# A four-stage transformer block on one core: one pool of eight PSUM banks in place of pools of five and three, with new due times for the planner

## The chip, the core and the metric

The kernel runs on one core of one Trainium2 chip. A core has a matrix engine (TensorE, PE in the profile, its weight loads shown apart as PEld), a vector engine (VectorE, DVE), a scalar engine (ScalarE, ACT), a general engine (GpSimd, POOL) and SyncE (SP), which here only issues DMAs. Each engine works through its own queue in order and waits for others by semaphores. TensorE writes its results to PSUM, which here is used as eight banks of 128 partitions by 512 fp32 values; VectorE and ScalarE read them from there. The metric is the device time of one launch in microseconds (us), taken as the median of several runs.

## The reference

The input x is 8 batches of 512 tokens by 512 features, in fp32. Four stages follow, each with the sandwich `x = x + layernorm(stage(layernorm(x)))`:

```
a0: scores = einsum('bci,bcj->bij', x, x); softmax; context = einsum('bij,bcj->bci', w, x)
f0: einsum('btd,rde->bte', x, factors) / sqrt(8) + bias          # factors: 8 of 512x512
a1: h = norm_scale * x / (rms(x) + eps) * split_scale
    q, k, v = h @ Wq.T, h @ Wk.T, h @ Wv.T       # 8 heads of 64, k and v for 2 groups
    x + softmax(q k^T / 8) v @ Wo.T
f1: g = (x @ gate_w.T) * gate_s;  u = (x @ up_w.T) * up_s         # 1408 wide, ternary weights
    (silu(g) * u) @ down_w.T * down_s
```

In f0 the eight factors act on the same input, so their sum is one matrix of 512x512.

## The kernel before

**Work and tiling.** A batch is four tiles of 128 tokens by 512 features. `layers` builds, for each of the eight batches, the operations of `stage_attn0` (a0), `stage_ffn0` (f0), `stage_attn1` (a1) and `stage_ffn1` (f1). The fp32 stages use fp32 matmuls. In f1 the weights are ternary and exact in the fp32r format, so each activation is split into two fp32r parts (`hl`, made by ScalarE at L1101 and VectorE at L1110), and both parts are multiplied (L1167 for gate and up, L1235 for down). At the start of the program the weights' low bits are tested (`look_at_low_bits`); with the given data a second, plain copy of the layers is skipped.

**Shapes of the array.** Most matmuls use the whole 128x128 array. Transposes of pairs of tiles (L637), transposes of attention weights (L977) and attention scores (L946) use 64-row halves of it, two at a time, and write two banks; the product of attention weights with v (L1008) uses 64-column halves. The program's names for these are "128x128", "128x128r" (fp32r), "64x128" and "128x64".

**The order.** `Recorder.add` takes each operation down with its engine, an estimated duration, what it reads and writes, and a due time. `Recorder.issue` then plays the whole program through: it keeps a clock for each engine and takes operations one at a time, and the order in which it takes them is the order in which they stand in the engines' queues on the chip. For each engine it looks at the operations that could start within `SLACK` of the earliest one, and takes the one with the lowest due time:

```
                pick = min(
                    (p + stay * self.change(e, state.get(e), op.state), n, s, op)
                    for s, p, n, op in able
                    if s <= first + slack[e]
                )
```

Here `change` is the planner's price of another array shape (on PE 0.21 us from "64x128" or "128x64" into "128x128r", 0.09 into any other, nothing between "128x128" and "128x128r") or of another function table (1.3 us on ACT), and it is part of the planned start `s` as well. `stay` is `STAY` of the engine. Due times are in units of one batch: `due` adds the stage's entry in `DUE`, the number of the batch, a `SHIFT` for the first three and last two batches, and a slope for each step within the stage (`e1` and `h1` are the attention and FFN of the last batch, which work in halves). `SMALL` is taken off the due time of operations under 0.3 us.

**Buffers.** A `Buf` gets a place of its tag when its first operation is taken, and gives it back when the last one is. If no place is free the operation can't be taken yet. PSUM has two tags: `f` with five banks, for a0, f0, a1, all transposes and one product of the half steps, and `g` with three, for gate, up and down products. Gate and up weights come in slices of 256 KB into four places of tag `wgu`, issued from POOL's queue (L389); x, factors and attention weights are issued from SP (L368). The product pair of one slice ends in a sigmoid on ScalarE (L1187) and two operations on VectorE (L1197, L1206), the last of which releases the second bank.

**Softmax.** A row takes VectorE's maximum (L575), ScalarE's exponential (L582), VectorE's reciprocal (L592) and its scaling (L599). A layernorm takes two statistics operations on VectorE (L518, L523), two small ones on POOL (L527, L534) and the normalisation on VectorE (L542).

Of the kernel before, what the change touches and what calls it, by code (L numbers as in the profile page):

```python
# [10 lines left out]
F32 = mybir.dt.float32  # L11
# [6 lines left out]
P = 128  # L18
# [35 lines left out]
class Recorder:  # L54
# [20 lines left out]
    def add(self, eng, dur, fn, reads=(), writes=(), room=(), after=(), state=None, lat=None):  # L75
# [5 lines left out]
        op.lat = self.LAT[eng] if lat is None else lat  # L81
        op.prio = self.prio - (SMALL if dur < 0.3 else 0.0)
        op.succ, op.wait, op.ready = [], 0, 0.0
# [34 lines left out]
    def issue(self, places, slack):  # L118
# [24 lines left out]
        while left:  # L143
            best = None
            for e, ops in ready.items():
# [3 lines left out]
                first = min(able)[0]  # L149
                stay = STAY.get(e, 0.0)  # L150
                pick = min(
# [99 lines left out]
def layers(  # L251
# [24 lines left out]
    B, S, D = x_in.shape  # L276
# [4 lines left out]
    NT = S // P  # L281
# [8 lines left out]
    psum = ctx.enter_context(tc.tile_pool(name="ps", bufs=1, space=bass.MemoryType.PSUM))  # L290
# [7 lines left out]
    def columns(tag, n, width):  # L298

        t = one(tag, [P, n * width])  # L300
        return [t[:, ts(i, width)] for i in range(n)]
# [21 lines left out]
        "ve": columns("ve", 24, 1),  # L323
        "rstd": columns("rstd", 24, 1),
        "s1": columns("s1", 24, 1),
        "f": [psum.tile([P, D], F32, tag=f"f{i}", name=f"f{i}") for i in range(5)],
        "g": [psum.tile([P, D], F32, tag=f"g{i}", name=f"g{i}") for i in range(3)],
    }
    ident = one("ident", [P, P])
    make_identity(nc, ident)  # L330
# [21 lines left out]
    def when(kind, b, *steps):  # L352

        rec.prio = due(kind, b if b < B // 2 else b - B, B, *steps)
# [17 lines left out]
    fsum = Fixed("fsum", BIG)  # L372
# [7 lines left out]
    wd = Fixed("wd", [P, NI, D], FAST)  # L380
# [125 lines left out]
    def whole(b):  # L506
        return (b, lambda t: t[:, :])
# [32 lines left out]
    def normalize(dst, src, mv, rstd, us=0.55, room=(), after=()):  # L540
        def go():
            nc.vector.tensor_scalar(  # L542
                ap(dst), ap(src), mv.t[:, 0:1], rstd.t[:, :], ALU.subtract, ALU.mult
            )

        add("DVE", us, go, reads=[ref(src), mv, rstd], writes=[ref(dst)], room=room, after=after)
# [570 lines left out]
    def stage_ffn1(x, b, after):  # L1117
# [11 lines left out]
        for q, (toks, its) in enumerate(rounds):  # L1129
            cut = slice(toks[0] * P, (toks[-1] + 1) * P)  # L1130
            mine = [(x_, (t, hf)) for x_ in xs for t in toks for hf in range(2)]
            took = (0.69, 0.75) if len(toks) == NT else (0.4, 0.42)
            for t in toks:
                if t in known:
                    continue
                known.add(t)
                when(kind + "norm", b, t - toks[0], q)
                if t % 2 == 0:
                    pair = [Buf("row"), Buf("row")]
                xn = pair[t % 2]  # L1140
                mv, rstd = moments(whole(x[t]))
                normalize(whole(xn), whole(x[t]), mv, rstd, room=[*xs, *pair])
                rows.append(whole(xn))
                if t % 2 == 0:
                    continue
                pts, into, bank = transpose_two(xs[0], t - 1, rows[-2:], room=xs, copy=False)
                for hf in range(2):
                    dsts = [((x_, (t, hf)), into(hf)) for x_ in xs]
                    in_parts(dsts, lambda hf=hf, bank=bank: bank(hf), [pts[hf]], 0.6, also=(t - 1, hf))

            for c, (lo, hi) in enumerate(CUTS):
                for it in range(lo, hi):
                    if it not in its:
                        continue
                    when(kind + "gate", b, it, q)
                    sig = Buf("sig" if len(toks) == NT else "e")
                    hd = (hds[c], lambda tt, k=it - lo, cut=cut: tt[:, k, cut])
                    pg, pu = Buf("g"), Buf("g" if len(toks) == NT else "f")
                    wg = load_slice("wgu", gate_t, it, after=after)
                    wu = load_slice("wgu", up_t, it, after=after)  # L1160

                    def product(bank, w, cut=cut):
                        def go():
                            n = 0
                            for kt in range(KT):
                                for d in xs:
                                    nc.tensor.matmul(  # L1167
                                        bank.t[:, cut],
                                        w.t[:, kt, :],
                                        d.t[:, kt, cut],  # L1170
                                        start=(n == 0),
                                        stop=(n == KT * len(xs) - 1),
                                    )
                                    n += 1

                        return go


                    us = PASS * KT * len(xs) * len(toks) / NT
                    mm(pg, us, product(pg, wg), [wg, *mine], room=[hds[c]], state=array)  # L1180
                    products.append(mm(pu, us, product(pu, wu), [wu, *mine], state=array))
                    gsc = lambda it=it: gs.t[:, it : it + 1]
                    usc = lambda it=it: us_.t[:, it : it + 1]
                    add(
                        "ACT",
                        took[0],
                        lambda sig=sig, pg=pg, gsc=gsc, cut=cut: nc.scalar.activation(  # L1187
                            sig.t[:, cut], pg.t[:, cut], AF.Sigmoid, scale=gsc()
                        ),
                        reads=[pg, gs],  # L1190
                        writes=[sig],
                        state="sig",
                    )
                    add(
                        "DVE",
                        took[1],
                        lambda sig=sig, pg=pg, gsc=gsc, cut=cut: nc.vector.scalar_tensor_tensor(  # L1197
                            sig.t[:, cut], pg.t[:, cut], gsc(), sig.t[:, cut], ALU.mult, ALU.mult
                        ),
                        reads=[pg, gs],  # L1200
                        writes=[sig],
                    )
                    add(
                        "DVE",
                        took[1],
                        lambda sig=sig, pu=pu, usc=usc, hd=hd, cut=cut: nc.vector.scalar_tensor_tensor(  # L1206
                            ap(hd), pu.t[:, cut], usc(), sig.t[:, cut], ALU.mult, ALU.mult
                        ),
                        reads=[pu, us_, sig],
                        writes=[(hds[c], (it - lo, u)) for u in range(2) if 2 * u in toks],  # L1210
                    )
        for t in range(NT):
            po = Buf("g")
            for c, (lo, hi) in enumerate(CUTS):
                when(kind + "down", b, t, c)
                n = hi - lo
# [55 lines left out]
    for b in range(B):  # L1272
        x = [Buf("x") for _ in range(NT)]
# [12 lines left out]
    with tc.manual_schedule():  # L1286
        rec.issue(places, SLACK)

# [1 line left out]


DUE = {
    "x": (-2.3159,),
    "fsum": (0.3241, 0.0093),
    "scales": (-1.7199,),
    "wd": (0.1588,),
    "low": (0.6749, 1.0396),
    "a0.norm": (0.5999,),
    "a0.row": (-0.0925, 0.0032),
    "a0.out": (0.61, 0.0014),  # L1300
    "f0": (-0.1636, 0.1196),
    "a1.norm": (0.4967, -0.0502),
    "a1.kv": (-1.8548,),
    "a1.q": (0.5431, 0.0591),
    "a1.row": (0.5193, 0.0765, 0.0294, -0.0187),
    "a1.mix": (1.4217, -0.005, 0.0185),
    "a1.out": (1.6212, -0.0623),
    "e1.row": (0.2868, -0.0014, 0.037, -0.0171),
    "e1.mix": (-2.6369, 42.9472, 0.5484),
    "e1.out": (1.0638, 0.0783, 0.0342),  # L1310
    "f1.norm": (-0.7064, 0.0727),
    "f1.gate": (1.5542, 0.001),
    "f1.down": (1.7443, 0.1972, 0.0317),
    "h1.norm": (1.3712, -0.2677, 0.0575),
    "h1.gate": (2.6762, 0.5726, 5.4087),
    "h1.down": (1.5597, -2.5384, 1.2861),
}

SHIFT = {
    ("a0", 0): -0.0077,  # L1320
    ("f0", 0): 0.3239,
    ("f1", 0): -0.0869,
    ("a0", 1): -0.1846,
    ("a1", 1): -0.1496,
    ("f0", 1): -0.3089,
    ("x", 1): -0.0564,
    ("a0", 2): 0.3238,
    ("a1", 2): -0.0022,
    ("f0", 2): 0.0353,
    ("f1", 2): -0.0044,  # L1330
    ("x", 2): 0.0586,
    ("a1", -2): -0.0031,
    ("f0", -2): 0.1802,
    ("f1", -2): -0.0946,
    ("x", -2): -0.3405,
    ("a0", -1): -0.0302,
    ("a1", -1): -0.1096,
    ("f0", -1): -0.4004,
    ("f1", -1): -0.1873,
    ("x", -1): 0.1371,  # L1340
}

STAY = {"PE": 0.0901}

SLACK = {"PE": 0.123, "ACT": 0.0528, "DVE": 0.0772, "POOL": 1.2606, "SP": 0.1357}

SMALL = 0.8159
FSUM_POOL = (0, 3)
EARLY = (-1,)
FEW = 4  # L1350
# [54 lines left out]
```

## Time and profile before

| | |
|---|---|
| median of 3 runs | 1515.19 us (1515.05 to 1517.9) |
| the profiled execution: its own time | 1514.31 us |
| the profiled execution: its span, first to last instruction | 1512.4 us |
| mean granted TensorE clock | 0.998 |
| PE busy | 1468.9 us |
| DVE busy | 1050.5 us |
| ACT busy | 665.7 us |
| POOL busy | 586.2 us |
| chain that ended last: share of PE | 86% |
| DMA moved | 108.04 MB |

Busy time of PE is the time in which at least one matmul is under way. Matmuls overlap at their ends, so that in a timeline the time that a group takes is read from its start to the start of the next one, not from its own length, which includes an end that runs beside the next. The kernel before is one that keeps PE busy for almost the whole span; the other engines have gaps.

### The profile page before, as it was taken

The numbers are of one execution on the slowest core, as the hardware profiler recorded it, in microseconds if no ns is written. First come the engines' busy times: TensorE is split into PE (matmuls) and PEld (weight loads), VectorE is DVE, ScalarE is ACT, GpSimd is POOL, SyncE is SP. The second block draws the span as 40 slices with busy tenths as digits, with TensorE's granted clock in tenths as the row PEclk, the third lists the DMA queues.
The fourth block names the chain that finished last, engine by engine and source line by source line (L and its number), as shares of the span: only waits on it lengthen the run. The fifth ranks groups of instructions, "written<-read, shape, count | busy, mean of one in ns | idle before, by whom it ended". The sixth has DMA issues, their size and how long they took to land.

```text
span 1512.4 us, 23159 instructions
## 1 busy us (share of the span) xinstructions
PE 1468.9 (97%) x8562; PEld 907.7 (60%) x8562; DVE 1050.5 (69%) x2227; ACT 665.7 (44%) x1422; POOL 586.2 (39%) x884
## 2 busy tenths in 40 slices
PE   5899999999999999999999999999999999999997
PEld 3444547765666556665576656665566655666575
DVE  6999875678567685586846868467774757758745
ACT  2225746441266423763246622465225652266412
POOL 6662132137512374033730347213571116611451
PEclk9999999999999999999999999999999999999999
DMA  9523124212431224212151122411233102420291
GB/s 336 158 82 108 29 64 97 50 57 58 85 68 43 46 53 97 51 42 71 28 106 35 57 56 47 101 36 43 57 70 84 36 15 63 88 59 29 49 168 38
DMA packets 156698, 108.04 MB, mean 71 GB/s; under 512 B 7072, under 2 KB 137120, under 8 KB 156576
## 3 DMA queue, kind: packets, MB, share of 16 engines
q0 software_dynamic: 98736, 51.13, 17.8%
q1 hardware_dynamic: 57840, 55.34, 11.9%
q8 instruction: 70, 1.15, 0.3%
q14 instruction: 52, 0.43, 0.1%
HBM read 98.06 MB, written 8.39 MB: 70 GB/s over the span
## 4 chain that ended last, share of the span: by engine, by line
PE 86%; DVE 5%; POOL 4%; issue 2%; DMA 1%; ACT 1%; SPq 0%; POOLq 0%; DVEq 0%; ACTq 0%
PE g L1167 21%; PE g L1235 11%; PE f L1008 8%; PE f L946 8%; PE f L917 7%; PE f L1034 7%; PE f L977 5%; PE f L726 5%; PE f L748 5%; PE f L695 4%; PE f L637 2%; PE f L898 2%; PE f L887 2%; POOL rstd L534 1%; DVE row L542 1%
## 5 line engine op out<-in xcount | busy, mean ns | idle before, releaser
L1167 PE MATMUL g<-hl,wgu 128*128 128x512 f32 (+1 forms) x1408 | 338.6, 394 | 2.7 <-DMA wgu<-in_gate_t 1.6
L1167 PEld LDWEIGHTS g<-hl,wgu 128*128 128x128 f32 x1408 | 256.0, 188 | 70.9 <-DVE s L575 10.6
L527 POOL TENSOR_SCALAR ve<-mv 128x1 f32<-128x1 f32 x224 | 67.8, 304 | 593.1 <-DVE mv L523 587.0
L575 DVE TENSOR_REDUCE s<-f 128x1 f32<-128x512 f32 x288 | 184.8, 683 | 97.7 <-PE f L946 57.2
L582 ACT ACTIVATE e<-f,s 128x512 f32<-128x512 f32 x288 | 196.0, 688 | 79.3 <-DVE s L575 76.2
L561 POOL TENSOR_TENSOR x<-x,z 128x512 f32<-128x512 f32 x120 | 165.3, 1382 | 47.0 <-DVE z L542 40.0
L1235 PE MATMUL g<-wd,hl 128*128 128x512 f32 x704 | 175.3, 402 | 1.4 <-DVE hl L1110 1.4
L989 ACT COPY big<-f 128x512 f32<-128x512 f32 x256 | 135.9, 593 | 80.6 <-PE f L977 80.1
L1235 PEld LDWEIGHTS g<-wd,hl 128*128 128x128 f32 x704 | 129.2, 188 | 52.1 <-issue 21.0
L599 DVE TENSOR_SCALAR e<-e,s 128x512 f32<-128x512 f32 x288 | 145.9, 511 | 8.2
L534 POOL TENSOR_TENSOR rstd<-ve,mhalf 128x1 f32<-128x1 f32 x224 | 143.7, 645 | 15.6
L389 POOL DMA_DIRECT2D wgu<-in_up_t x92 | 74.0, 804 | 158.7 <-PE g L1167 157.0
L946 PE MATMUL f<-kv,big 64*128 64x512 f32 x512 | 129.8, 614 | 0.4 <-ACT e L582 0.4
L1008 PE MATMUL f<-big,kv 128*64 128x256 f32 x1024 | 122.9, 385 | 0.0
L1197 DVE SCALAR_TENSOR_TENSOR sig<-g,gs,sig 128x512 f32<-128x512 f32 x84 | 62.8, 748 | 85.7 <-ACT sig L1187 85.6
L1206 DVE SCALAR_TENSOR_TENSOR hd<-g,us,sig 128x512 f32<-128x512 f32 x84 | 62.8, 747 | 82.9 <-PE g L1167 81.1
L917 PE MATMUL f<-big,ws 128*128 128x512 f32 x256 | 115.9, 599 | 0.8 <-DVE z L761 0.7
L1034 PE MATMUL f<-ws,big 128*128 128x512 f32 x256 | 116.2, 599 | 0.0
L748 PE MATMUL f<-fsum,rT 128*128 128x512 f32 x256 | 115.4, 594 | 0.1
L726 PE MATMUL f<-big,big 128*128 128x512 f32 x256 | 115.0, 598 | 0.0
L977 PEld LDWEIGHTS f<-ident,e 64*128 64x128 f32 x2048 | 73.3, 139 | 52.5 <-issue 40.7
L389 POOL DMA_DIRECT2D wgu<-in_gate_t x92 | 73.0, 793 | 80.9 <-PE g L1167 76.9
(91 smaller groups left out, 1896.9 us busy)
## 6 DMA issues: line engine op xcount, KB each, us to landing
wgu<-in_gate_t POOLq DMA_DIRECT2D x92, 256.0 KB, 3.4
wgu<-in_up_t POOLq DMA_DIRECT2D x92, 256.0 KB, 3.4
x<-in_x SPq DMA_DIRECT2D x32, 256.0 KB, 2.7
ws<-in_wq_t SPq DMA_DIRECT2D x32, 256.0 KB, 3.3
ws<-in_wo_t SPq DMA_DIRECT2D x32, 256.0 KB, 2.6
out<-x SPq DMA_DIRECT2D x32, 256.0 KB, 2.0
hd<-in_factors SPq DMA_DIRECT2D x28, 256.0 KB, 5.3
wd<-in_down_t POOLq DMA_DIRECT2D x11, 256.0 KB, 8.4
```

The source lines that it names most:

```text
L534: lambda: nc.gpsimd.tensor_tensor(rstd.t[:, :], ve.t[:, :], mhalf, ALU.pow),
L561: lambda: on.tensor_tensor(ap(xt), ap(xt), y.t[:, :], ALU.add),
L575: lambda: nc.vector.tensor_reduce(nmax.t[:, :], sc.t[:, :], AX.X, ALU.max, negate=True),
L582: lambda: nc.scalar.activation(e.t[:, :], sc.t[:, :], AF.Exp, bias=nmax.t[:, :], accum_out=tot.t[:, :]),
L726: nc.tensor.matmul(po.t[:, :], xnT.t[:, j, ts(t, P)], wT.t[:, j, :], start=(j == 0), stop=(j == KT - 1),)
L748: nc.tensor.matmul(po.t[:, :], xnT.t[:, kt, :], fsum.t[:, kt, :], start=(kt == 0), stop=(kt == KT - 1),)
L917: nc.tensor.matmul(pq.t[:, :], wq.t[:, kt, :], hT.t[:, kt, :], start=(kt == 0), stop=(kt == KT - 1),)
L946: nc.tensor.matmul(scs[g].t[:, :], qT.t[gp, i, ts(s, P)], kT.t[gp, :], start=True, stop=True,)
L1008: nc.tensor.matmul(po.t[gp, : 2 * P], v.t[:, t * P + g * DH : t * P + (g + 1) * DH], columns_of(aT)[:, g * NT + t, :], start=(t == 0), sto ...
L1034: nc.tensor.matmul(po.t[:, :], qT.t[:, i, ts(t, P)], flat(wos[i].t), start=(i == 0), stop=(i == NPAIR - 1),)
L1167: nc.tensor.matmul(bank.t[:, cut], w.t[:, kt, :], d.t[:, kt, cut], start=(n == 0), stop=(n == KT * len(xs) - 1),)
L1235: nc.tensor.matmul(po.t[:, :], ap(o)[:, it - lo, :], wd.t[:, it, :], start=(it == 0 and k == 0), stop=(it == NI - 1 and k == len(ops) - 1),)
```

## The change

The two lists of banks become one of eight, and everything that took a `g` takes an `f`. All entries of `DUE`, most of `SHIFT`, and `STAY`, `SLACK` (but SP's) and `SMALL` have new values. Nothing is added to or taken from the operations; their order on the engines' queues is the planner's to make from the new numbers.

```diff
-        "f": [psum.tile([P, D], F32, tag=f"f{i}", name=f"f{i}") for i in range(5)],
-        "g": [psum.tile([P, D], F32, tag=f"g{i}", name=f"g{i}") for i in range(3)],
+        "f": [psum.tile([P, D], F32, tag=f"f{i}", name=f"f{i}") for i in range(8)],
...
-                    pg, pu = Buf("g"), Buf("g" if len(toks) == NT else "f")
+                    pg, pu = Buf("f"), Buf("f")
...
-            po = Buf("g")
+            po = Buf("f")
...
-    "x": (-2.3159,),
-    "fsum": (0.3241, 0.0093),
-    "scales": (-1.7199,),
-    "wd": (0.1588,),
-    "low": (0.6749, 1.0396),
-    "a0.norm": (0.5999,),
-    "a0.row": (-0.0925, 0.0032),
-    "a0.out": (0.61, 0.0014),
-    "f0": (-0.1636, 0.1196),
...
-    "a1.row": (0.5193, 0.0765, 0.0294, -0.0187),
-    "a1.mix": (1.4217, -0.005, 0.0185),
-    "a1.out": (1.6212, -0.0623),
...
-    "f1.gate": (1.5542, 0.001),
-    "f1.down": (1.7443, 0.1972, 0.0317),
-    "h1.norm": (1.3712, -0.2677, 0.0575),
-    "h1.gate": (2.6762, 0.5726, 5.4087),
-    "h1.down": (1.5597, -2.5384, 1.2861),
+    "x": (-2.7683,),
+    "fsum": (0.2458, 0.047),
+    "scales": (-0.966,),
+    "wd": (-1.0342,),
+    "low": (1.4453, 0.9619),
+    "a0.norm": (0.5635,),
+    "a0.row": (0.4046, 0.0015),
+    "a0.out": (1.079, 0.0003),
+    "f0": (0.0108, 0.1903),
...
+    "a1.row": (0.5464, 0.097, 0.1452, 0.002),
+    "a1.mix": (1.4399, 0.0087, 0.0208),
+    "a1.out": (1.5638, -0.0514),
...
+    "f1.gate": (1.4971, 0.0171),
+    "f1.down": (1.7065, 0.0786, 0.0706),
+    "h1.norm": (1.3749, -0.0528, 0.2791),
+    "h1.gate": (3.2517, 0.1751, 4.9204),
+    "h1.down": (2.657, -0.7693, 0.3197),
...
-    ("a0", 0): -0.0077,
-    ("f0", 0): 0.3239,
...
-    ("x", 1): -0.0564,
...
+    ("a0", 0): -0.6388,
+    ("a1", 0): 0.2026,
+    ("f0", 0): 0.0621,
...
+    ("x", 0): 0.011,
...
-STAY = {"PE": 0.0901}
+STAY = {"PE": 0.7688}
-SLACK = {"PE": 0.123, "ACT": 0.0528, "DVE": 0.0772, "POOL": 1.2606, "SP": 0.1357}
+SLACK = {"PE": 0.091, "ACT": 0.3013, "DVE": 0.0546, "POOL": 0.7933, "SP": 0.1357}
-SMALL = 0.8159
+SMALL = 0.5354
```

More of the change, by code (lines that the diff above doesn't have):

```diff
@@ L1292 @@
 DUE = {
-    "x": (-2.3159,),
-    "fsum": (0.3241, 0.0093),
-    "scales": (-1.7199,),
-    "wd": (0.1588,),
-    "low": (0.6749, 1.0396),
-    "a0.norm": (0.5999,),
-    "a0.row": (-0.0925, 0.0032),
-    "a0.out": (0.61, 0.0014),
-    "f0": (-0.1636, 0.1196),
-    "a1.norm": (0.4967, -0.0502),
-    "a1.kv": (-1.8548,),
-    "a1.q": (0.5431, 0.0591),
-    "a1.row": (0.5193, 0.0765, 0.0294, -0.0187),
-    "a1.mix": (1.4217, -0.005, 0.0185),
-    "a1.out": (1.6212, -0.0623),
-    "e1.row": (0.2868, -0.0014, 0.037, -0.0171),
@@ L1309 @@
-    "e1.mix": (-2.6369, 42.9472, 0.5484),
-    "e1.out": (1.0638, 0.0783, 0.0342),
-    "f1.norm": (-0.7064, 0.0727),
-    "f1.gate": (1.5542, 0.001),
-    "f1.down": (1.7443, 0.1972, 0.0317),
-    "h1.norm": (1.3712, -0.2677, 0.0575),
-    "h1.gate": (2.6762, 0.5726, 5.4087),
-    "h1.down": (1.5597, -2.5384, 1.2861),
+    "x": (-2.7683,),
[5 more added lines that the diff above has]
+    "a0.row": (0.4046, 0.0015),
@@ new lines @@
+    "a0.out": (1.079, 0.0003),
+    "f0": (0.0108, 0.1903),
+    "a1.norm": (0.1225, -0.0316),
+    "a1.kv": (-1.1559,),
+    "a1.q": (0.5146, 0.2023),
+    "a1.row": (0.5464, 0.097, 0.1452, 0.002),
+    "a1.mix": (1.4399, 0.0087, 0.0208),
+    "a1.out": (1.5638, -0.0514),
+    "e1.row": (0.4703, 0.0117, 0.0577, -0.2992),
+    "e1.mix": (-2.1799, 34.298, 0.0605),
+    "e1.out": (1.0442, 0.0079, 0.5004),
+    "f1.norm": (-0.1784, 0.4817),
+    "f1.gate": (1.4971, 0.0171),
+    "f1.down": (1.7065, 0.0786, 0.0706),
@@ L1317 @@
+    "h1.norm": (1.3749, -0.0528, 0.2791),
+    "h1.gate": (3.2517, 0.1751, 4.9204),
+    "h1.down": (2.657, -0.7693, 0.3197),
 }
 SHIFT = {
-    ("a0", 0): -0.0077,
-    ("f0", 0): 0.3239,
[L1322 to L1325, printed above, removed]
-    ("x", 1): -0.0564,
[L1327 to L1340, printed above, removed]
-}
-STAY = {"PE": 0.0901}
-SLACK = {"PE": 0.123, "ACT": 0.0528, "DVE": 0.0772, "POOL": 1.2606, "SP": 0.1357}
-SMALL = 0.8159
+    ("a0", 0): -0.6388,
+    ("a1", 0): 0.2026,
+    ("f0", 0): 0.0621,
+    ("f1", 0): -0.0607,
+    ("x", 0): 0.011,
+    ("a0", 1): -0.1334,
+    ("a1", 1): 0.0419,
+    ("f0", 1): -0.0031,
+    ("f1", 1): 0.0014,
+    ("a0", 2): 0.0621,
@@ L1348 @@
+    ("f0", 2): -0.0014,
+    ("x", 2): 0.2224,
+    ("a1", -2): -0.0049,
+    ("f0", -2): -0.0369,
+    ("x", -2): -0.1583,
+    ("a1", -1): 0.3168,
+    ("f0", -1): -0.0577,
+    ("f1", -1): 0.2403,
+    ("x", -1): -0.1214,
+}
+STAY = {"PE": 0.7688}
+SLACK = {"PE": 0.091, "ACT": 0.3013, "DVE": 0.0546, "POOL": 0.7933, "SP": 0.1357}
+SMALL = 0.5354
 FSUM_POOL = (0, 3)
```

## The prediction

> **What bounds the kernel now.** I read four views in turn. First the page's busy times, then the same by stretch of time (columns: stretch, its length, busy us of PE, PEld, DVE, ACT and POOL, granted clock, DMA share, GB/s).
>
> ```profile
> PE 1468.9 (97%) x8562; PEld 907.7 (60%) x8562; DVE 1050.5 (69%) x2227; ACT 665.7 (44%) x1422; POOL 586.2 (39%) x884
> ```
>
> ```profile
> 0.00:20.00 20.00, 4.08 (x20) 2.42 (x21) 11.13 (x26) 2.36 (x3) 13.19 (x37) 1.00 0.99 315
> 20.00:50.00 30.00, 28.10 (x155) 15.40 (x155) 25.32 (x41) 11.50 (x27) 17.46 (x18) 1.00 0.97 325
> 50.00:100.00 50.00, 44.23 (x197) 22.56 (x196) 44.38 (x94) 11.74 (x31) 36.92 (x59) 1.00 0.24 69
> ...
> 1400.00:1450.00 50.00, 47.26 (x350) 30.86 (x349) 35.85 (x78) 17.86 (x38) 24.77 (x38) 1.00 0.44 86
> ...
> 1503.00:1513.00 10.00, 0.00 (x0) 0.00 (x0) 2.50 (x5) 0.00 (x0) 0.79 (x2) 0.59 0.14 51
> ```
>
> ```profile
> 682.55:864.80 182.25, 182.05 (x1065) 112.47 (x1063) 123.76 (x271) 84.00 (x179) 70.78 (x106) 1.00 0.26 59
> 864.80:1047.05 182.25, 182.05 (x1064) 112.46 (x1062) 123.56 (x271) 84.06 (x179) 70.80 (x106) 1.00 0.26 58
> ```
>
> PE is idle for 1512.4 - 1468.9 = 43.5 us, and nearly all of it lies at the ends: 15.9 before the first transpose, 1.9 in 20:50, 5.8 in 50:100, 2.7 in 1400:1450, about 10 after the last matmul. In the middle the same stretch of 182.25 us (a batch) repeats with 0.2 us idle. So nothing waits for data there; a faster order can only cut what PE spends when it is *busy*. That is the third view, PE's timeline (start, length, instructions):
>
> ```profile
> 868.14 0.71 PE L977 MATMUL f<-ident,e 64*128 64x64 f32 x16
> 868.78 3.70 PE L1034 MATMUL f<-ws,big 128*128 128x512 f32 x8
> 872.41 0.71 PE L977 MATMUL f<-ident,e 64*128 64x64 f32 x16
> ...
> 881.31 3.60 PE L1034 MATMUL f<-ws,big 128*128 128x512 f32 x8
> 884.74 0.38 PE L693 MATMUL f<-ident,u 128*128 128x128 f32 x2
> ```
>
> ```profile
> 968.46 5.73 PE L1167 MATMUL g<-hl,wgu 128*128 128x512 f32 x24
> 974.13 1.21 PE L977 MATMUL f<-ident,e 64*128 64x64 f32 x32
> 975.27 3.70 PE L917 MATMUL f<-big,ws 128*128 128x512 f32 x8
> 978.90 1.99 PE L946 MATMUL f<-kv,big 64*128 64x512 f32 x8
> 980.82 5.74 PE L1167 MATMUL g<-hl,wgu 128*128 128x512 f32 x24
> 986.48 1.21 PE L977 MATMUL f<-ident,e 64*128 64x64 f32 x32
> ```
>
> Take start to start. The same projection takes 872.41 - 868.78 = 3.63 us between 64-row transposes and 884.74 - 881.31 = 3.43 between 128-row work: 0.20 more, plus about 0.15 on the 64-row neighbours (a 16-instruction transpose takes 0.64 with another shape on both sides, 0.55 or 0.59 with one on one side, so 0.50 with none). A run of 24 FFN products takes 5.67, one of 40 (940.45 to 949.79) 9.33, so 1.83 per eight, and 5.67 - 3 x 1.83 = 0.18 for entering and leaving it, again plus 0.15 next door. Between 128-row work a visit to the FFN's fp32r products costs about nothing (what the visit loses the neighbour gains). So **a change of array shape costs about 0.165 us**. The steady batch has 61 changes of kind, 12 of them between 128-row fp32 and fp32r; 49 x 0.165 = 8.1 us of 182.25. Over the run it is 395 shape changes, some 65 us. With the 43.5 idle, about 109 us is all that an order can touch; it can't get near that.
>
> Here a rule must be weighed. The Trainium skill ("Trainium Kernel Development and Optimization", section Best Practices) says to judge the distance to the roofline by the weight loads' busy share and not by the matmuls'. The loads are at 60%, so by it some 600 us would be open. The row for one form, 3.43 us for eight instructions wherever its neighbours don't change, says that an fp32 product streams for 0.429 us whatever its 0.19 us load does; none of that gap is an order's to win. I use the rows: at most 109.
>
> **The change, part by part.**
>
> *Banks.* No instruction is added or removed; the matmuls, evictions and DMAs are the same. FFN products (L1167), down products (L1235) and attention draw from eight banks in place of three and five. The trace shows where three bind: both runs above stop at 24 instructions, three products, the size of g, as ACT is at exponentials until 972.6 and reads the first product only at 973.87. PE then does other work, so the limit costs two shape changes (0.33 us), not idle time. With eight banks such a run can go on.
>
> *STAY 0.0901 to 0.7688.* This weighs the planner's price of a change (0.21 from a half-array shape into fp32r, 0.09 for any other, 0 between fp32 and fp32r on the whole array) in units of a batch. A change of 0.09 is worth 0.0081 batch before (1.5 us of due time) and 0.069 after (12.6 us). PE will leave the whole array for a slightly more urgent 64-row operation far less often. Out of a half-array shape the PE slack counts too: with 128-row work ready at 0.09, fp32r at 0.21 lay within 0.123 of it before and lies outside 0.091 after, so FFN work will follow 128-row work, where its entry is free, rather than 64-row work.
>
> *Due times in the middle.* f1.gate 1.554 to 1.497 stands now ahead of the next batch's first attention rows (1.519 to 1.546); a0.out goes from 0.61 to 1.079, behind f1.gate and f1.down of the batch before. Both make FFN runs longer. How many changes fall away no row tells. Of ten FFN visits beside 64-row work in a batch, merging the two 24-runs with their 16- and 8-instruction neighbours takes out two, 0.66 us; one 128-row visit fewer between transposes takes 0.35. I take 1.0 us a batch. Bounds: 3.0 (nine of ten visits merged), and -1.0 (six changes more, where the new due times spread the attention steps out). Six steady batches and about one more in the run-in and run-out: **-7 us**, bounds -21 and +7. The freed time is PE's own, so no cover is needed; but softmax then finds longer FFN runs between its steps, and what is late next is VectorE's maximum (L575), for which ScalarE's exponential waits 76.2 us in total already, off PE's path.
>
> *The head.* Batch 0 by sums: x -2.316 to -2.757, wd 0.159 to -1.034, a0.norm 0.592 to -0.075, fsum 0.324 to 0.246, scales -1.720 to -0.966. On SP the eight tiles of x now go ahead of the two small scale loads (2.59 to 3.5 us now); on POOL all eleven wd issues (0.567 each, 6.2 us) go ahead of the small variance operations that slip between them now, and the four power operations that started at 11.91 stay behind them. The first normalisation starts at 15.34, held not by them but by VectorE's queue: four statistics of the next batch stand before it, and their tiles land 1.36 us apart with the DMA engines at 0.99. Those stay in front in the new order too. I take -0.5 there (bounds -3 and +2), and -1 for the 5.8 us in 50:100, where VectorE is 89% busy and normalisation and rows of batch 0 now go ahead of the factor sums (bounds -5, if all of it goes, and +4, if the sums come late for L748, which PE needs from 62 us on). **-1.5.**
>
> *The tail.* The last batch's halves (h1, e1) get new due times; 4.9 us of idle in 1400:1503 could shrink or double, and the 10 us after the last matmul (a statistics chain and one store) is no order's to change. **0**, bounds -4 and +5.
>
> *SLACK, SMALL, loads.* They reorder engines of 39 to 69% load whose waits PE doesn't see; 0 while that holds. The cover is PE's queue of ready work: weight slices land 3.4 us after issue and cost PE 1.6 us in the whole run.
>
> Sum: 1514.31 (the profiled execution: span 1512.4 and 1.9 around it) - 7 - 1.5 = 1505.8. The median of the runs, 1515.19, is 0.9 above that execution: **1507**.
>
> **The rivals.**
>
> *Crowded banks (slower).* Three banks were FFN's and five attention's; now a run of products may hold most of the eight while ScalarE is at exponentials. A scores or transpose step needs two banks at once; it would wait for a second read by VectorE (L1206, 0.747 us) behind a sigmoid (0.694). Here the skill speaks against the change: "TensorEngine Tiling (Array Packing)", section Restrictions and Gotchas, has row tiling raise the pressure on PSUM, since each row tile writes to a bank of its own. In the trace PE waits for banks hardly at all under the split; by the rule, four waits of 0.75 us per batch in seven batches make +21, so 1507 + 21 = 1528. It decides from 8.5 us on, 1.6 such waits a batch. For it: attention uses its five banks fully (two double score steps stand at 978.90 to 980.82). Against: the planner knows of banks, and would place other work.
>
> *Ends get worse.* The middle gains 3, while head and tail go to their upper bounds, 2 + 4 + 5 = 11: 1515 + 11 - 3 = 1523. For it: these steps have little work beside them. Against: their chains, not the due times, set much of their length.
>
> *No gain.* The order turns over but a batch keeps about 49 shape changes, and PE is as full as before: 1515 (1512.2 to 1518.2).
>
> *More than that.* Over a third of a batch's changes go, 3 us by seven, and the head gives 1: 1493.
>
> **How the numbers follow.** This kernel's runs tell about 0.2% (3 us) from no change. Fewer changes as forecast, 1507, own range 1499 to 1512: 0.45. More, 1493: 0.07. No gain: 0.12. Crowded banks, 1519 to 1540: 0.24. Worse ends, 1519 to 1527: 0.12. So faster 0.52, same 0.12, slower 0.36. The range 1496 to 1529 leaves out most of the 1493 case and the upper half of the crowded one, 0.17.
>
> **What would show it.** A steady batch near 181.2 us, with fewer than 49 shape changes, and runs of L1167 longer than 24 among attention; PE idle there still under 0.5 us. Crowding would show as idle PE ahead of L946, L977 or L1167, ended by VectorE or ScalarE. Worse ends would show as a first matmul after 16 us, or over 6 us idle in 50:100. The forecast is wrong if the batch is at 182.25 or above.

## The result

The changed kernel takes **1497.0 us** (median of 4 runs, 1495.49 to 1497.7) where the kernel before takes 1516.15 beside it: ratio 0.9876, 95% interval 0.9863 to 0.9888. It is 19 us faster where 8 were forecast. The profiled execution took 1497.16, its span is 1495.3, 17.1 below the span before. In the file the line numbers of all stages are one lower than before (L1166 is the FFN product, L1234 the down product, L976, L945 and L1007 the attention operations).

The busy times of the changed kernel, from its profile:

```profile
span 1495.3 us, 23054 instructions
...
PE 1451.0 (97%) x8562; PEld 903.7 (60%) x8562; DVE 1073.7 (72%) x2227; ACT 637.6 (43%) x1406; POOL 576.9 (39%) x884
```

PE's busy time fell by 1468.9 - 1451.0 = 17.9 us with the same 8562 instructions, and its idle time went from 43.5 to 44.3. Over the whole run the gain is busy time, as forecast; the section after this one shows that idle time fell at the start and rose in the middle by about as much. The same stretches as in the prediction (stretch, length, busy us of PE, PEld, DVE, ACT, POOL, clock, DMA share, GB/s):

```profile
0.00:20.00 20.00, 5.60 (x23) 2.96 (x24) 9.47 (x23) 2.36 (x3) 12.31 (x36) 1.00 1.04 321
20.00:50.00 30.00, 26.06 (x145) 14.56 (x144) 26.56 (x46) 11.49 (x27) 21.24 (x21) 0.89 0.98 332
50.00:100.00 50.00, 49.83 (x216) 25.43 (x215) 44.06 (x97) 11.99 (x32) 38.67 (x63) 1.00 0.22 63
...
570.71:752.39 181.68, 179.91 (x1063) 112.01 (x1063) 129.34 (x270) 80.49 (x176) 69.41 (x106) 1.00 0.26 59
752.39:934.05 181.66, 179.88 (x1063) 112.01 (x1063) 129.35 (x270) 80.49 (x176) 69.36 (x106) 1.00 0.26 59
```

A steady batch takes 181.67 us in place of 182.25: 2.15 less of PE busy, but 1.78 idle in place of 0.20. And 50:100 is now full, where 5.8 us were idle; 20:50 has 3.9 idle in place of 1.9, and its granted clock is 0.89. PE's timeline in the attention of a steady batch (start, length, operation, number of instructions):

```profile
788.98 3.70 PE L916 MATMUL f<-big,ws 128*128 128x512 f32 x8
792.11 6.05 PE L1166 MATMUL f<-hl,wgu 128*128 128x512 f32 x24
798.09 1.21 PE L976 MATMUL f<-ident,e 64*128 64x64 f32 x32
799.14 1.94 PE L945 MATMUL f<-kv,big 64*128 64x512 f32 x8
801.00 3.70 PE L916 MATMUL f<-big,ws 128*128 128x512 f32 x8
804.14 3.37 PE L1234 MATMUL f<-wd,hl 128*128 128x512 f32 x12
807.44 1.21 PE L976 MATMUL f<-ident,e 64*128 64x64 f32 x32
808.48 1.94 PE L945 MATMUL f<-kv,big 64*128 64x512 f32 x8
```

Two transpose steps (L976 x32) and two score steps (L945 x8) follow one another: four steps of 64-row work in one visit, each writing two banks, eight in all. Before, L977 x32 and L946 x8 had 128-row or FFN work between them. And most of the FFN's runs now follow 128-row work, where the entry is free: of 15 FFN visits in a batch 4 begin after half-array work, before it was 10 of 16. A steady batch has 36 changes of array shape in place of 49, the whole run 303 in place of 395.

### The profile page after: what moved, and what is told of

Its sections match the earlier page's. It is cut to its first block, busy times and chain, and to the rows that moved or that the text cites. A ratio compares the mean times of both kernels' runs of the same rounds, so it can differ in the third digit from the quotient of the medians.

```text
span 1495.3 us, 23054 instructions
## 1 busy us (share of the span) xinstructions
PE 1451.0 (97%) x8562; PEld 903.7 (60%) x8562; DVE 1073.7 (72%) x2227; ACT 637.6 (43%) x1406; POOL 576.9 (39%) x884
## 4 chain that ended last, share of the span: by engine, by line
PE 79%; DVE 10%; POOL 6%; issue 3%; DMA 2%; SPq 0%; ACT 0%; POOLq 0%; DVEq 0%; ACTq 0%
PE f L1166 17%; PE f L1234 11%; PE f L1007 8%; PE f L945 8%; PE f L916 8%; PE f L1033 5%; PE f L976 5%; PE f L694 4%; PE f L747 4%; PE f L725 3%; DVE st L517 2%; POOL rstd L533 2%; PE f L897 2%; PE f L886 2%; POOL wgu L388 1%
## 5 line engine op out<-in xcount | busy, mean ns | idle before, releaser
L1166 PE MATMUL f<-hl,wgu 128*128 128x512 f32 (+1 forms) x1472 | 348.6, 391 | 3.8 <-DMA wgu<-in_gate_t 2.2
L1166 PEld LDWEIGHTS f<-hl,wgu 128*128 128x128 f32 x1472 | 265.8, 188 | 69.5 <-issue 15.1
L560 POOL TENSOR_TENSOR x<-x,z 128x512 f32<-128x512 f32 x120 | 160.5, 1343 | 53.0 <-DVE z L541 44.2
L1234 PE MATMUL f<-wd,hl 128*128 128x512 f32 x704 | 179.1, 407 | 1.4 <-DVE hl L1109 1.4
L598 DVE TENSOR_SCALAR e<-e,s 128x512 f32<-128x512 f32 x288 | 158.0, 549 | 9.3
L1234 PEld LDWEIGHTS f<-wd,hl 128*128 128x128 f32 x704 | 130.5, 188 | 49.5 <-issue 15.2
L1186 ACT ACTIVATE sig<-f,gs 128x512 f32<-128x512 f32 x84 | 57.9, 690 | 217.2 <-PE f L1166 147.8
L533 POOL TENSOR_TENSOR rstd<-ve,mhalf 128x1 f32<-128x1 f32 x224 | 139.9, 628 | 15.5
L945 PE MATMUL f<-kv,big 64*128 64x512 f32 x512 | 127.4, 609 | 0.0
L1007 PE MATMUL f<-big,kv 128*64 128x256 f32 x1024 | 121.3, 384 | 0.9 <-ACT big L988 0.9
L1205 DVE SCALAR_TENSOR_TENSOR hd<-f,us,sig 128x512 f32<-128x512 f32 x84 | 62.9, 749 | 80.7 <-PE f L1166 78.1
L1196 DVE SCALAR_TENSOR_TENSOR sig<-f,gs,sig 128x512 f32<-128x512 f32 x84 | 62.8, 747 | 79.6 <-ACT sig L1186 79.6
L1007 PEld LDWEIGHTS f<-big,kv 128*64 128x64 f32 x1024 | 69.2, 137 | 58.7 <-ACT big L988 17.6
```

The lines of the kernel that those rows point to most:

```text
L533: lambda: nc.gpsimd.tensor_tensor(rstd.t[:, :], ve.t[:, :], mhalf, ALU.pow),
L560: lambda: on.tensor_tensor(ap(xt), ap(xt), y.t[:, :], ALU.add),
L945: nc.tensor.matmul(scs[g].t[:, :], qT.t[gp, i, ts(s, P)], kT.t[gp, :], start=True, stop=True,)
L1007: nc.tensor.matmul(po.t[gp, : 2 * P], v.t[:, t * P + g * DH : t * P + (g + 1) * DH], columns_of(aT)[:, g * NT + t, :], start=(t == 0), sto ...
L1166: nc.tensor.matmul(bank.t[:, cut], w.t[:, kt, :], d.t[:, kt, cut], start=(n == 0), stop=(n == KT * len(xs) - 1),)
L1234: nc.tensor.matmul(po.t[:, :], ap(o)[:, it - lo, :], wd.t[:, it, :], start=(it == 0 and k == 0), stop=(it == NI - 1 and k == len(ops) - 1),)
```

## Where the time went

To divide the run I give each matmul instruction its shortest spacing in the traces (0.429 us for an fp32 one of 512 columns, 0.228 for an FFN product, and so on); they sum to 1392 us. At the point where 200 us of this work are done (soon after the FFN of batch 0 begins) the run is cut in two. "Time" is up to there, and from there to the last matmul; the last column is what is neither work nor idle, mostly the changes.

| kernel | head: time | changes | idle | rest: time | changes | idle | other |
|---|---|---|---|---|---|---|---|
| before | 247.3 | 70 | 27.6 | 1255.4 | 325 | 6.1 | 57.0 |
| changed | 236.7 | 65 | 20.0 | 1248.9 | 238 | 14.6 | 42.0 |
| old order on eight banks | 245.7 | 70 | 26.7 | 1255.4 | 325 | 6.9 | 56.1 |
| changed, changes put back | 237.1 | 71 | 20.2 | 1257.0 | 302 | 12.5 | 52.2 |
| changed, old STAY | 239.4 | 67 | 23.3 | 1267.2 | 267 | 22.3 | 52.6 |
| changed, old wd | 246.9 | 63 | 26.2 | 1248.6 | 238 | 14.2 | 42.1 |
| changed, old f0 shift | 241.8 | 65 | 23.0 | 1248.5 | 238 | 14.4 | 41.8 |
| searched again | 237.4 | 63 | 21.6 | 1240.7 | 247 | 7.3 | 41.1 |

So the 17.1 us are **10.6 in the head** and **6.5 in the rest**, and the 6.5 are 87 fewer changes worth 15.0 less 8.5 of new idle time.

The table does not show the clock. In the profiles the granted clock is 1.00 but for stretches at 0.50, which come after a longer stop of PE or several short ones. The changed kernel has one while PE works: 6.8 us from 32.7 us on, after a stop of 3.8 us. The kernel before has none until its last matmul is done. Half of PE's busy time in such stretches is my estimate of what they cost: 3.2 us here. The length varies between executions of one kernel (the one with changes put back has 6.8 us in one profile and 3.4 in another). The rest ran at full clock in both kernels, so the 15.0 and the 8.5 are free of it.

Of the head's 10.6 us, then, 7.6 are idle time (27.6 to 20.0) and five changes are worth 0.8, while the half clock takes 3.2 back. The 5.4 that remain are neither; the next section finds 1.4 of them.

## The experiments

**The banks alone.** The theory: fewer changes of array shape. The rival: more banks by themselves, since a result need not wait for its bank to be read. The old plan is made with its five and three, and then laid out in the same order with results going to whichever of eight banks has been free longest (`plan` is the old `issue`, which here only notes the order):

```diff
+        order = self.plan(places, slack)
...
+        free["f"] = free["g"] = [(0.0, i, t) for i, t in enumerate(places["f"] + places["g"])]
+        for n, op in enumerate(order):
+            for b in op.bufs:
+                if b.t is None:
+                    _, _, b.t = free[b.tag].pop(0)
+            op.fn()
...
```

> The order of the kernel before is kept instruction by instruction (395 shape changes); only the bank that each result goes to comes from one list of eight, the one free longest. If fewer shape changes made the gain, nothing changes: 1516 us, within 3. If more banks by themselves made it (less waiting for a bank to be read), the time falls towards 1497, at least to 1511.

Measured: 1510.77 us (1509.59 to 1511.6) beside 1516.02, ratio 0.9968 (0.9955 to 0.998). Some 5 us: more than the theory allowed (within 3), and just what the rival named as its least (1511), but much less than the 19. One profiled execution, with an expectation of its own:

> A look at where the 5.3 us of the old order on eight banks come from. If they are waits for a bank to be read, PE has fewer stops on ScalarE and VectorE at the same 395 shape changes: idle time falls from 43.5 by about 4 to 5 us (most of it in the head, 50:100, where 5.8 us are idle) and PE's busy time stays at 1468.9, within 1.5. If it is something else, busy time falls.

This execution took 1512.63 us, span 1510.8. Idle is 43.4 and busy 1467.5, so the first expectation missed: no idle time went. Put beside the old trace, instruction by instruction (the order on PE is the same), all of the 1.6 us arises between 57 and 230 us, where batch 0 has little beside it; from there to the end the two run level within 0.7. The head of this execution also has two half-clock stretches of 3.4 us (from 61.6 and 170.8), by the same estimate 3.4 us lost that the trace of before has not; without them it would be an estimated 5.0 us ahead, about the difference of the timed runs. Part of it can be seen, and it is a wait for a bank that no idle time shows. The same score step of batch 0, before and on eight banks (L964 in that file):

```profile
163.50 1.60 PE L946 MATMUL f<-kv,big 64*128 64x512 f32 x4 [0.39 <-ACT e L582]
```

```profile
160.86 1.08 PE L964 MATMUL f<-kv,big 64*128 64x512 f32 x4
```

Before, its second half starts 0.48 us after its first, released by ScalarE's copy (L989) out of a bank; PE counts as busy meanwhile. On eight banks the halves start 0.005 us apart. Three score steps of the kernel before are parted so (at 163.5, 172.4 and 180.9 us), by 1.4 us in all, and none here or in the changed kernel. In the steady batches the banks changed nothing: the rest takes 1255.4 us in both. So banks without a new order are worth about 5 us, in the head.

**The new numbers without the banks, and the banks without the new numbers.** First the changed kernel with its banks split again, for the copy of the layers that runs; the down product gets `Buf(GT)` too:

```diff
+    GT = "g" if split else "f"
...
-        "f": [psum.tile([P, D], F32, tag=f"f{i}", name=f"f{i}") for i in range(8)],
+        "f": [psum.tile([P, D], F32, tag=f"f{i}", name=f"f{i}") for i in range(5 if split else 8)],
+        "g": [psum.tile([P, D], F32, tag=f"g{i}", name=f"g{i}") for i in range(3 if split else 0)],
...
-                    pg, pu = Buf("f"), Buf("f")
+                    pg, pu = Buf(GT), Buf(GT if len(toks) == NT else "f")
```

> The changed kernel's due times, STAY, SLACK and SMALL on the old split of five and three. The planner's order then has 402 shape changes. If the new numbers made the gain and banks are a detail, it stays under 1510. If the order lives on eight shared banks, PE's idle time rises by far more than the changes cost (99 x 0.165 = 16): 1560 or above.

Measured: 1658.04 us (1656.62 to 1659.43), ratio 1.0942 (1.0924 to 1.096). PE's idle time is 142.0 us, 97.7 more than in the changed kernel, and 63.3 of it are twelve waits of the transposes for a normalised row. Busy time is 63 more: 99 changes at 0.165 are 16, and half-clock stretches cost an estimated 27 more than in the changed kernel; the other 20 stay open. The other half of the question, the kernel before with `f` of eight banks and its old numbers:

> The kernel before with one pool of eight banks and all its old numbers. The order has 371 shape changes, 24 fewer. If more banks by themselves help the planner, 1516 - 24 x 0.165 - 5 = 1507. If the old due times only fit the split, the order falls apart and idle time of PE makes it slower than 1530.

Measured: 1576.62 us (1574.45 to 1578.37), ratio 1.04 (1.0382 to 1.0419). Its waits of PE, the longest in total first (engine, line, what it waited for: us, times, longest):

```profile
PE f L636 <- DVE row L541: 24.6, 8, 9.5
PE f L610 <- DVE row L541: 18.7, 6, 13.1
PE f L636 <- DVE big L541: 15.8, 1, 15.8
```

This order has 24 changes fewer than the one before and is 61.5 us slower. PE is idle for 94.7 us, 51 more; 43.3 of them are waits for a normalised row (the first two lines). Busy time rose by 12.4 although changes fell away, and half-clock stretches cost an estimated 18 of it. The numbers and the pool only work together. The reading, which is argued: a free pool lets the planner take operations in another order, and due times that fit the split then leave PE without ready work.

**One bank fewer.** `range(7)` in place of `range(8)`:

> The changed kernel with seven banks. The planner's order has 343 shape changes, 40 more: 1497 + 40 x 0.195 = 1504.8 if only the count matters. If the new order needs the eighth bank to keep PE fed, PE's idle time rises as well, by 10 us or more, and the time is 1515 or above. If banks do not matter, 1497.

Measured: 1537.47 us (1535.71 to 1538.77), ratio 1.0144 (1.0127 to 1.0161), 40 over the changed kernel. Its profile (1537.03 us) tells most of it. PE's idle time is 65.3 us, 21.0 more, so the expectation's second case came true. Of this 14.0 is a single stop for a normalised row of f0, and the clock is then at half from 554.0 to 571.1 us, so that the eight instructions behind it take 6.6 us to the next start (571.70), where 3.43 is usual:

```profile
563.25 1.11 PE L610 MATMUL f<-ident,row 128*128 128x128 f32 x4 [14.04 <-DVE row L541]
565.10 6.67 PE L747 MATMUL f<-fsum,rT 128*128 128x512 f32 x8 [0.73 <-ACT rT L614]
```

Busy time rose by 18.9: the 40 changes are 6.6 of it at 0.165, and half-clock stretches an estimated 7 more than in the changed kernel. The remaining 5 stay open.

**The price of a change.** In the changed kernel's order 35 operations on PE are moved ahead of earlier ones of another shape, at places where their inputs are due by then. Buffers are dealt out again along the new order; the operations stay:

```diff
...
+        for late, early in EXCHANGED if len(self.ops) == COUNT else ():
+            op = self.ops[late]
+            order.remove(op)
+            order.insert(order.index(self.ops[early]), op)
...
+EXCHANGED = [
+    (438, 436), (500, 967), (589, 1002), (1055, 710), (730, 1072), (1069, 744),
...
```

> The order of the changed kernel, in which 35 operations on PE go ahead of one neighbour (or more) of another shape, where their inputs are due by then; banks, due times and all instructions stay. It puts back 70 shape changes (373 in place of 303). If changes of shape are the cause, PE's busy time rises by 70 x 0.165 to 70 x 0.195 us = 11.6 to 13.7, and the time is 1508.5 to 1510.7. If the gain lies in the ends or in earlier inputs, and a change costs nothing, it stays at 1497, within 3.

Measured: 1506.45 us (1505.47 to 1506.86), 9.5 above the changed kernel and 2 short of the range for this theory. One profiled execution:

> A look at the changed kernel with 70 shape changes put back (1506.45 in the timed runs, 9.5 over). If all of it is the price of a change, busy time is 1451.0 + 9 to 12 and idle stays at 44.3, within 2.

```profile
PE 1461.4 (97%) x8562; PEld 903.2 (60%) x8562; DVE 1074.8 (71%) x2227; ACT 639.8 (43%) x1406; POOL 574.9 (38%) x884
```

Busy time rose by 10.4, which is 0.148 us a change. This execution has 3.4 us at half clock where the changed kernel's has 6.8, an estimated 1.6 us less lost; with that counted it is 0.17. In the table's rest, where both ran at full clock, it is 52.2 - 42.0 over 64 changes, 0.159. From before to changed it is 15.0 over 87, 0.172, and in a steady batch 2.15 over 13, 0.165. The theory stands. Idle time fell by 1.8, which is why the time missed its range: a steady batch has 1.1 of it in place of 1.8. Why was not tried.

**STAY.**

> The changed kernel with STAY 0.0901 as before. The planner's order then has 334 shape changes, 31 more. If the count is all: 1497 + 31 x 0.195 = 1503. If STAY made most of the gain, 1510 or more, and the rest beyond 6 us shows as idle time of PE, since the due times were not searched for this value.

Measured: 1519.33 us (1516.79 to 1523.66), ratio to before 1.0023 (1.0016 to 1.0031). One profiled execution:

> A look at the changed kernel with the old STAY (334 shape changes, 1519.33 in the timed runs, 22 over). The 31 changes are worth 31 x 0.15 to 0.165 = 4.7 to 5.1 us of busy time; the other 17 us should be idle time, 44.3 + 15 to 19, if the new due times only keep PE fed together with the new STAY.

This execution took 1518.19. Idle is 55.4, 11 more and not 17; busy is 1461.0, 10 more, of which 31 changes explain 5; the half clock costs as much as in the changed kernel. The other 5 are not the changes'; waits too short to part two matmuls, whose ends overlap in the record, would count so, but this run does not separate them. A steady batch takes 184.2 us with 41 changes and 2.7 idle. So STAY alone takes 5 of the 13 changes back per batch; the remaining 8 come with the pool and the due times.

**The head.** Two single numbers whose return upsets only the first two batches. First wd:

```diff
-    "wd": (-1.0342,),
+    "wd": (0.1588,),
```

> The changed kernel with the due time of wd as before (0.1588 in place of -1.0342), all else new. The planner's order has 301 shape changes, two fewer, so by the count nothing changes: 1497. If the head's gain comes from how the first two batches are laid out, and this one number upsets it, the steady batch stays at 181.7 us and the head loses 5 to 8 us again: 1502 to 1505, all of the loss before the first long FFN run (225 us).

Measured: 1506.64 us (1505.51 to 1506.94), 9.6 over, somewhat more than expected. By the table all of it is in the head (246.9 against 236.7), and the rest is level to 0.3 us. PE's waits there, first of this kernel, then of the changed one:

```profile
PE f L636 <- DVE big L541: 9.1, 1, 9.1
PE f L610 <- DVE row L541: 7.9, 1, 7.9
```

```profile
PE f L636 <- DVE big L541: 14.4, 1, 14.4
PE f L636 <- DVE e L598: 3.8, 1, 3.8
```

With wd late, POOL does batch 0's variances between the wd issues and PE begins at 9.1 us, 5.3 earlier. It then runs out of work at 53 us and stands for 7.9 until f0 of batch 0 has its first row. After that stop the clock is at half until 68.8 us: f0's first product takes 6.46 us from start to start, the next 3.53.

```profile
62.82 6.62 PE L747 MATMUL f<-fsum,rT 128*128 128x512 f32 x8 [0.77 <-ACT rT L614]
69.28 0.60 PE L610 MATMUL f<-ident,row 128*128 128x128 f32 x4
```

The row is normalised after layernorm powers (L533) that stand on POOL behind the additions to the factor sum, and the last of these ends at 55.2 us in this kernel, at 54.2 in the changed one: both load the factors with the DMA engines at 0.95 to 1.05 until 50 us. So an earlier start of PE does not bring the row. At 30 us of work this kernel is 9.4 us ahead of the changed one, at 40 it is 3.4 behind: 8.7 of the 12.8 are idle time and about 3.5 the half clock. Some 7 us more are lost between 80 and 140 us of work. Then the shift of f0 in batch 1:

```diff
-    ("f0", 1): -0.0031,
+    ("f0", 1): -0.3089,
```

> The changed kernel with the shift of f0 in batch 1 as before (-0.3089 in place of -0.0031), all else new, 303 shape changes. By the count 1497. If the head's gain is one of layout (work of batch 1 kept back to fill the softmax waits of batch 0's attention), 1503 to 1506, the loss between 130 and 240 us and idle or waiting time of PE there.

Measured: 1501.97 us (1499.95 to 1504.15), 5.0 over; the table has 5.1 of it in the head, and it arises between 120 and 200 us of work, that is from 150 us on. There batch 0's attention waits for its softmax (PE's waits for scaled rows, L598, come to 2.2 us in 100:250, where the changed kernel has 0.6), and a kernel that has kept f0 of batch 1 back has something to put between. Both results fit one reading, which is argued and not shown: what counts is which work of batches 0 and 1 is left when PE needs a filler.

**A plan without the new idle time.** The new idle time of a steady batch, 1.78 us, lies at two places, both ended by VectorE (waits of PE in 570:935, two batches):

```profile
PE f L636 <- DVE e L598: 1.9, 2, 1.0
PE f L610 <- DVE row L541: 1.6, 2, 0.8
```

The first is one slow operation. VectorE's scaling of a row (L598) is planned at 0.48 us; its mean of 0.549 hides that most take 0.49 and this one 3.02:

```profile
875.46 3.02 DVE L598 TENSOR_SCALAR e<-e,s 128x512 f32<-128x512 f32 x1
875.69 2.49 POOL L560 TENSOR_TENSOR x<-x,z 128x512 f32<-128x512 f32 x2
878.53 0.46 PE L636 MATMUL f<-ident,e 64*128 64x64 f32 x8 [0.96 <-DVE e L598]
```

GpSimd (POOL) makes two additions beside it. Of the 288 scalings 245 have no arithmetic of GpSimd beside them, and none of these takes over 0.49 us. The same happens in five batches (at 512.2, 693.8, 875.5, 1057.1 and 1238.8 us). That the additions hold the scaling up was not tried by a run of its own. The normalisations are planned at 0.55 us and take 0.56 to 0.81 in the trace of before (the mean, by what they read). So I searched on from the changed kernel's numbers, judging each order with the durations of the traces; the kernel differs from the changed one in its numbers only:

```diff
...
-    "a0.out": (1.079, 0.0003),
-    "f0": (0.0108, 0.1903),
+    "a0.out": (1.2854, 0.0244),
+    "f0": (-0.0873, 0.1869),
...
-    "a1.kv": (-1.1559,),
+    "a1.kv": (-0.5489,),
...
-STAY = {"PE": 0.7688}
-SLACK = {"PE": 0.091, "ACT": 0.3013, "DVE": 0.0546, "POOL": 0.7933, "SP": 0.1357}
-SMALL = 0.5354
+STAY = {"PE": 0.625}
+SLACK = {"PE": 0.0933, "ACT": 0.2833, "DVE": 0.0595, "POOL": 0.9203, "SP": 0.0712}
+SMALL = 1.2902
```

> New due times, searched from those of the changed kernel with the durations that the traces show (0.165 us for every change of array shape, 0.55 for the scaling of a softmax row, 0.65 for a normalisation, 1.37 for POOL's additions), so that VectorE's real times are planned for. 310 shape changes, 7 more. If the new stall of 1.6 us a batch comes from VectorE being planned too fast, idle time of PE in a steady batch falls from 1.8 to under 1 us and the time is 1486 to 1493. If the stall has another cause, 1497 or above.

Measured: **1489.85 us** (1489.59 to 1490.18), ratio to before 0.9831 (0.9814 to 0.9847), 7 below the changed kernel. Its steady batches:

```profile
559.20:738.90 179.70, 179.70 (x1064) 112.20 (x1063) 129.04 (x271) 80.80 (x178) 70.21 (x108) 1.00 0.27 60
738.90:918.60 179.70, 179.70 (x1064) 112.21 (x1063) 128.99 (x271) 80.83 (x177) 69.91 (x107) 1.00 0.27 60
```

No idle time is left in them, with 37 changes a batch, and the longest scaling in them takes 1.5 us. The expectation (1486 to 1493, under 1 us idle) came true: the stall could be planned away. All numbers changed at once, so the run does not show that the durations alone did it.

## Why the prediction was right or wrong

- **What bounds the kernel, and the price of a change** (0.165 us): right. 13 changes fewer cut 2.15 us of busy time from a steady batch, and putting changes back cost 0.15 to 0.17 each. To use the rows and not the weight loads' share held too: PEld stayed at 60% while the time fell. (The section cited there names a second measure, MFU, beside the loads' share; the forecast weighed the loads' share alone.)
- **How many changes fall away** ("I take 1.0 us a batch", six changes): too small by half; it was 13. The way was partly wrong as well. I had FFN runs merging; 15 of 16 FFN visits remain. What merged is 64-row work, two transposes and two scores in one visit, which takes all eight banks, and FFN visits moved beside 128-row work. The second was in the prediction's part on STAY and the PE slack, without a number.
- **"PE idle there still under 0.5 us"**: wrong, 1.78. That the cover holds (waits of the other engines that "PE doesn't see") failed here: a scaling of a0's rows that took 3.02 us beside GpSimd's additions, and a normalisation, were late for PE's transposes. The two errors cancel, 15.0 against 8.5, so the rest came to -6.5 beside the forecast -7: right in size by luck.
- **The head** (-1.5): this is the step that failed, and it made the forecast miss. It was -10.6, beyond the bounds of -3 and -5 together. In 50:100, of whose 5.8 us idle I took 1, 5.6 went (20:50 gave 2.0 back). And I sized the term by the waits of 0:20 and 50:100 and by operations of batch 0 alone, and left out 100:250, where batch 0's attention has little beside it: of the 10.6, the first 120 us of work give 4.2, the next 80 give 6.4. I also gave more banks nothing there, since PE was hardly idle for them; the old order on eight banks is worth about 5 us, part of it waits inside score steps that count as busy. Of the numbers that I argued from, the old value of x or of fsum, put back by itself, gives the same program, and that of scales only moves two small loads. wd, taken as part of -0.5, costs 9.6 when put back, and not through the first matmul. This and the 5.0 of f0's shift come to more than the 10.6, so they are no shares of it. Where the head's time fell is shown; why just this layout fills it stays in part open.
- **The tail** (0): right, 0.7 us longer after 1330 us of work.
- **Crowded banks**: not seen. No wait of PE ahead of the scores (L945) is in the changed kernel's list, no score step is parted, and its transposes of attention weights (L976) waited 0.6 us in all, for a scaled row and not for a bank. The caution of the Trainium skill ("TensorEngine Tiling (Array Packing)", Restrictions and Gotchas) that row tiling presses on PSUM agrees with the kernel before, where three score steps waited for the second of their two banks, and with the timeline above, where four steps of 64-row work write all eight. With seven banks the same numbers cost 40 us and with five and three 161, but the longest waits of PE there are for normalised rows.

## What to carry to other kernels

When an engine is busy all the time, count what its busy time is made of. Here each change of array shape costs about a sixth of a microsecond, and in the steady batches eight shared banks paid off by letting like work stand together, not by removing waits. A plan that was searched for one set of buffers cost 40 to 161 us on another: judge them as one change. Size the start of a program by the stretches in which work runs out, not by the moment in which the engine starts. And look at the clock before a difference in busy time is explained: here a stop of 7.9 us was followed by an estimated 3.5 us lost at half clock.

## What was not expected

The kernel in which the matrix engine starts 5.3 us earlier is the slower one (9.1 us to the first matmul in a run of 1506.94, 14.4 in one of 1497.16). And a visit to fp32r between fp32 matmuls on the whole array is free within 0.02 us. In the kernel before:

```profile
926.43 3.59 PE L748 MATMUL f<-fsum,rT 128*128 128x512 f32 x8
929.46 4.21 PE L1167 MATMUL g<-hl,wgu 128*128 128x512 f32 x16
933.50 0.60 PE L611 MATMUL f<-ident,row 128*128 128x128 f32 x4
```

The 16 FFN instructions begin 3.03 us after the fp32 product, 0.40 earlier than its usual 3.43, and take 4.04 to the next start, 0.38 more than two times 1.83: 7.07 in all in place of 7.09.
